# A recurrent step of seven Strassen products: one x block per pair of steps, and h handed on by quadrants

## The chip, the cores and the metric

One core of a Trainium2 chip runs the whole program in one launch. The metric is the device time of one execution in microseconds; the kernel before was measured three times. Engines: TensorE (PE, with its weight loads PEld) does matmuls into PSUM; VectorE (DVE), ScalarE (ACT) and GpSimd (POOL) do the rest; SyncE (SP) only issues DMAs here. Each engine takes its instructions in order.

## What is computed

Two layers, each with its residual. For 64 sequences, 256 steps and width 1024:

```
xW = x @ Wx + b                        # (64, 256, 1024)
h_t = tanh(h_{t-1} @ Wh + xW[:, t])    # h_{-1} = cond, 256 steps one after another
x = x + h
gate = sigmoid(silu(cond @ W1.T + b1) @ W2.T + b2)
x = x + (x + IHaar(gate * Haar(x)))    # the transform over the steps, and its inverse
```

The gate is one row per sequence, the same for all steps, so the transform is undone by its inverse and the second layer comes to x * (2 + gate). The kernel computes `(x + h) * factor` with `factor` = 2 + gate, step by step. All is float32.

## The kernel before

**Layouts.** There are 64 sequences in two groups of 32. A step's h is held "naturally" as 128 partitions x 512 (partition: a quarter q of the width and a sequence within its group; columns: group and 256 of the width), and transposed, `hT`, as the stationary operand of matmuls. A quadrant is 128 columns (E) of these 512: index 0 to 3 for the blocks a11, a12, a21, a22 of a 2 x 2 split of h. An x tile holds a pair of steps (S = 2) and all 64 sequences, transposed.

**h @ Wh** is one level of Strassen-Winograd: seven products of quadrants by blocks of Wh that are prepared once (`StrassenWeight`). `strassen_sides` makes the four sums s0 to s3 of quadrants of `hT` on VectorE (L223 to L226). `strassen_product(out, a, i)` (L182 to L201) issues product i: 4 k by 4 column tiles, 16 float32 matmuls that the profile shows as 32 records, on line 193. `h_product` issues them in the order 1, 2, 5, 6, 7, 4, 3. Products 2, 4, 3 accumulate on a PSUM bank `acc` that ScalarE has filled with the step's xW (`put`, L235); the sums `y` and `u` of the others come off the banks `m16` and `m57` by ScalarE (L246, L251) and VectorE (L257, L260). Then, for the whole 512 columns at once, VectorE adds `h = acc + y` (L265), ScalarE takes tanh (L499), VectorE transposes (L500) and makes the sides of the next step.

**x @ Wx** (`XWork`) is done for a pair of steps at a time, each float32 operand split into three parts of fewer bits, with 48 matmuls of 512 columns (line 278): 16 into the banks `mixed0`, `mixed1` (x2 by wx2), 32 into `main0`, `main1` (x1 by wx1, x0 by wx0). Of these, 24 stand behind the products of an odd step (`first`: 16 mixed and 8 main) and 24 behind those of the even step after it (`second`). The split is VectorE's (L119 high bits, L298 x1, L300 x2) and ScalarE's (L306, x0). `take_mixed` brings `mixed` to SBUF by ScalarE (L314) and adds the bias by GpSimd (L315); `finish` adds `main` by VectorE (L352), writes the sum to DRAM (`sum_d`, L356) and reads it back in the layout of h with eight DMAs (`xw`, L362), all issued by SP.

**The rest of a step.** GpSimd adds hT to the x tile (L562) and multiplies by `factor` (L462); after the odd step SP stores the tile (L586) and loads a later x (L115). The first five pairs come before `factor` is known: they are parked in DRAM (`kept`), and brought back, multiplied and stored later, one half tile in eight steps (`again`).

**The last steps.** The pair 127 gets its xW by plain float32 products in the layout of h, in four pieces beside steps 251 to 254 (`tail_step`, from the weights that `raw_again` puts together again on VectorE), and the last two steps are handled in halves (`pieces`) and added to x and multiplied by VectorE in the transposed layout.

**What sets the order.** TensorE's instructions are issued in the order of the program all through (`manual_schedule`); those of VectorE and ScalarE up to step 1, after which a planner orders them, GpSimd and SP by its own costs. DMAs issued by SP wait for their data in SP's queue, so a waiting one holds those behind it.

Of the kernel before, what the change touches and what calls it, by code (L numbers as in the profile page):

```python
# [52 lines left out]
F32 = mybir.dt.float32  # L53
# [7 lines left out]
P = 128  # L61
R = 32
# [10 lines left out]
HIGH = -(1 << 12)  # L73
UP = float(1 << 12)
DOWN = 1.0 / UP
WARM = 9
LATE = 3
AHEAD = 2
RINGS = 1024


@with_exitstack
def tile_cond_resid(
    ctx: ExitStack,
    tc: tile.TileContext,
    xT: bass.AP,
    condT: bass.AP,
    wx: bass.AP,
    wh: bass.AP,
# [130 lines left out]
    def strassen_sides(hT, t: int):  # L220
        a11, a12, a21, a22 = (hT[:, i * E : (i + 1) * E] for i in range(4))
        s = sums.tile([P, 4, E], F32, tag="s", name=f"s{t}")
        nc.vector.tensor_sub(s[:, 2], a11, a21)  # L223
        nc.vector.tensor_add(s[:, 0], a21, a22)  # L224
        nc.vector.tensor_sub(s[:, 1], s[:, 0], a11)  # L225
        nc.vector.tensor_sub(s[:, 3], a12, s[:, 1])  # L226
        return {1: a11, 2: a12, 3: s[:, 3], 4: a22, 5: s[:, 0], 6: s[:, 1], 7: s[:, 2]}
# [10 lines left out]
    def h_product(acc, a: dict, t: int):  # L238

        m16, m57 = (bank(f"m{i}", f"m{i}_{t}") for i in (16, 57))  # L240
        m16, m5, m7 = m16[:, :E], m57[:, :E], m57[:, E : 2 * E]
        part = [acc[:, i * E : (i + 1) * E] for i in range(3)]
        y = sums.tile([P, 4, E], F32, tag="y", name=f"y{t}")
        u = sums.tile([P, E], F32, tag="u", name=f"u{t}")
        strassen_product(m16, a[1], 1, True)
        nc.scalar.copy(y[:, 0], m16)  # L246

        strassen_product(part[0], a[2], 2) if t != S else None
        strassen_product(m5, a[5], 5, True)
        strassen_product(m16, a[6], 6)  # L250
        nc.scalar.copy(u, m16)  # L251
        strassen_product(m7, a[7], 7)
        strassen_product(part[0], a[2], 2) if t == S else None
        if t == 1:
            for k in range(B - 2, B):
                gate_block(k)
        nc.vector.tensor_add(  # L257
            y[:, 1:3], m57[:, : 2 * E].rearrange("p (i e) -> p i e", i=2), u[:].unsqueeze(1).broadcast_to((P, 2, E))
        )
        nc.vector.tensor_add(y[:, 3], m7, y[:, 1])  # L260
        strassen_product(part[2], a[4], 4)
        strassen_product(part[1], a[3], 3)
        h = work.tile([P, W], F32, tag="h", bufs=1, name=f"h{t}")
        for v in pieces(t):
            nc.vector.tensor_add(h[:, v], acc[:, v], flat(y)[:, v])  # L265
        return h

    def pieces(t: int) -> list:


        return [slice(F, W), slice(0, F)] if t + S >= T else [slice(0, W)]

    def bank(tag: str, name: str):
        return one_pool.tile([P, HALF], F32, tag=tag, name=name)
# [11 lines left out]
    class XWork:  # L286
# [14 lines left out]
                out=self.x2, in0=self.x1[:].bitcast(F32), scalar=-UP, in1=self.high, op0=ALU.mult, op1=ALU.add  # L301
            )

        def begin(self) -> None:
            self.x0 = split.tile([P, D], F32R, tag="x0", name=f"x0_{self.i}")
            nc.scalar.copy(self.x0, self.high)  # L306
            self.mixed = [bank(f"mixed{h}", f"mixed{h}_{self.i}") for h in range(2)]
            self.main = [bank(f"main{h}", f"main{h}_{self.i}") for h in range(2)]

# [7 lines left out]
        def block(self, k: int) -> None:  # L317
# [5 lines left out]
            for h in range(2):  # L323
                x_matmul(self.main, self.x1, 1, h, k, stop=True)

        def first(self) -> None:
            self.begin()

            def low() -> None:
                for k in range(B):  # L330
                    x_matmul(self.main, self.x1, 1, 0, k, start=True)


            low() if self.i == 2 else None
            for h in range(2):
                for k in range(B):
                    x_matmul(self.mixed, self.x2, 2, h, k, True, True)
            self.take_mixed()
            low() if self.i > 2 else None
# [79 lines left out]
    for k in range(B):  # L419
        x_block(k)  # L420
        split_block(k)
        if k == 0:
            now = XWork(1)
            now.split()
            now.begin()
        if k in (3, 5):
            now.block(k // 4)
# [13 lines left out]
        return g1T  # L441

    def gate_factor(z):
        nc.vector.tensor_add(z, gate_ps, z)
        nc.scalar.activation(z, z, AF.Sigmoid)
        factor = const.tile([P, W], F32, tag="factor", name="factor")
        nc.vector.transpose(factor, z)
        nc.vector.tensor_scalar_add(factor, factor, 2.0)  # L448
        return factor
# [15 lines left out]
    nc.vector.tensor_add(h, acc, b_n)  # L465

    tail = {T - 5: [range(3)] * 2, T - 4: [range(3, 5)] * 2, T - 3: [range(5, B), []], T - 2: [[], range(5, B)]}  # L470
    wx_again, ends = [], []

    def raw_again(k: int) -> None:
        wx_again.append(wpool.tile([P, D], F32, tag="wx2", name=f"wx_again{k}"))
        w0, w1 = (wx_s[k][j][:].bitcast(F32) for j in range(2))
        tc.keep_in_program_order(
            nc.vector.scalar_tensor_tensor(out=wx_again[k], in0=w1, scalar=DOWN, in1=w0, op0=ALU.mult, op1=ALU.add)
        )

    def tail_step(t: int) -> None:  # L480
        if not ends:
            for r in range(S):
                ends.append(bank(f"mixed{r}", f"acc{T - S + r}"))
                nc.scalar.copy(ends[r], b_end)
        for r, ks in enumerate(tail[t]):
            for k in ks:
                plain_product(ends[r], pairs[NP - 1], wx_again[k], k, lambda g: (k * S + r) * N + g * R, False, False)


    kept, again, factor = [], [], None  # L490
    for t in range(T):
        i, s = divmod(t, S)
        if s == 0 and t:
            xw = xw_next
        if t:
            h = h_product(acc, sides, t)
        hT = work.tile([P, W], F32, tag="hT", name=f"hT{t}")
        for v in pieces(t):
            nc.scalar.activation(h[:, v], h[:, v], AF.Tanh)  # L499
            nc.vector.transpose(hT[:, v], h[:, v])  # L500
        if t + 1 < T:
            sides = strassen_sides(hT, t)
        if t == 0:
            acc = bank("acc", "acc1")
            nc.vector.tensor_add(acc, acc1, b_n)
# [15 lines left out]
            later.split()  # L521

        elif s == 0:
            if i + 1 < NP:
                acc = put(xw[1], t + 1)
            if i + 2 < NP:
                now.second()
                if i + 3 < NP:
                    later = XWork(i + 2)
                    later.split()  # L530
                xw_next = now.finish()
        if s == 1 and i + 3 < NP:
            now = later
            now.first()
        if s == 1 and i + 2 < NP:
            acc = put(xw_next[0], t + 1)
        if t in tail:
            tail_step(t)

        if T - 7 <= t < T - 3:  # L540
            for k in ((0, 1, 2), (3, 4), (5, 6), (7,))[t - T + 7]:
                raw_again(k)
        if t == T - 16:
            b_end = load_bias(b.rearrange("o (q f) -> (o q) f", q=Q), const, "spare", "b_end")
        if t >= T - 3 and t < T - 1:
            acc = ends[t - T + 3]
        if t == 1:
            in_order.close()
        if t == 2:
# [5 lines left out]
        if t == 0:  # L555
            hT0 = hT
        elif t == 1:

            for r, v in enumerate((hT0, hT)):
                tc.keep_in_program_order(nc.gpsimd.tensor_add(of_step(x, r), of_step(x, r), blocks(v)))  # L560
        elif t + S < T:
            nc.gpsimd.tensor_add(of_step(x, s), of_step(x, s), blocks(hT))  # L562
        if LATE <= t < LATE + B:
            k = t - LATE
# [3 lines left out]
            nc.sync.dma_start(out=w2, in_=w2T[k])  # L568
            plain_product(gate_ps, g1T, w2, k)
            if k == B - 1:  # L570
                factor = gate_factor(b2_n)
        if t + S >= T:

            if s == 0:
                last = slab("last")
            for g, queue in zip((1, 0), (nc.scalar, nc.sync)):
                v = of_step(x, s)[:, g]
                nc.vector.tensor_add(v, v, blocks(hT)[:, g])
                part = slice(s * W + g * F, s * W + (g + 1) * F)
                out = last[:, part].rearrange("p (b m) -> p b m", b=B)  # L580
                nc.vector.tensor_mul(out, v, blocks(factor)[:, g])
                queue.dma_start(out=yT[i][:, part], in_=last[:, part])
        elif factor is not None:
            scale(x, s)
            if s == S - 1:
                nc.sync.dma_start(out=yT[i], in_=x)  # L586
        elif s == S - 1:
            kept.append(dram.tile([P, D], F32, tag="kept", bufs=(LATE + B) // S, name=f"kept{i}"))
            nc.sync.dma_start(out=kept[i], in_=x)
        if s == S - 1:  # L590
            del pairs[i]
            if i + 3 < NP:
                load_x(i + 3)


        if t >= 2 * B and t % 4 == 3 and kept:
# [8 lines left out]
                tc.keep_in_program_order(nc.sync.dma_start(out=by_block, in_=at(kept[j])))  # L605
            else:
                v = again[:].rearrange("p (b g m) -> p g b m", b=B, g=G)
                tc.keep_in_program_order(nc.gpsimd.tensor_mul(v, v, blocks(factor)))
                nc.sync.dma_start(out=at(yT[j]), in_=by_block)
                if (j + 1, r + 1) == (len(kept), S):  # L610
                    kept = []
# [31 lines left out]
```

## Time and profile before

| | us |
|---|---|
| median of three runs | 3089.21 (3089.11 to 3089.31) |
| the profiled execution, device time | 3086.83 |
| its span, first to last instruction | 3085.0 |
| TensorE busy | 3077.1 |
| VectorE busy | 1763.5 |
| GpSimd busy | 1113.6 |
| ScalarE busy | 714.2 |
| half a pair (one step and 24 x matmuls), median of 228 | 11.913 |

A timeline row is: start in us from the span's start, length in us, engine, line, operation, output tile <- input tiles, shapes, count; in brackets the idle time of the engine before it and what ended it. Consecutive instructions of one kind are merged into one row. A matmul's end is modelled, so rows of matmuls overlap; their starts tell the pace. A group row (by line) gives busy time and mean length in ns, then the idle time in front and its releaser.

### The profile page before, as it was taken

How to read it: one execution, taken by the hardware profiler on the slowest of the kernel's cores; microseconds unless marked ns; L12 is line 12 of the kernel's file. 1: busy time of each engine (PE TensorE's matmuls, PEld its weight loads, DVE VectorE, ACT ScalarE, POOL GpSimd, SP SyncE). 2: the span in 40 equal slices, each digit the busy share in tenths (PEclk: the TensorE clock that was granted, in tenths of full speed). 3: DMA queues.
4: the chain of work that ended last, by engine and by line, in shares of the span. 5: the costliest groups of instructions: out<-in, count | busy, mean ns of one | idle time of the engine just before them, and what ended most of it. 6: DMA issues, size and time to landing. Idle time of an engine off the chain costs nothing.

```text
span 3085.0 us, 138204 instructions
## 1 busy us (share of the span) xinstructions
PE 3077.1 (100%) x64073; PEld 2691.3 (87%) x64073; DVE 1763.5 (57%) x2740; ACT 714.2 (23%) x1420; POOL 1113.6 (36%) x764
## 2 busy tenths in 40 slices
PE   9999999999999999999999999999999999999999
PEld 6888888888888888888888888888888888888888
DVE  7555555555555555555555555555555555555556
ACT  3222222222222222222222222222222222222221
POOL 2233343334333333333333334333333333333332
PEclk9999999999999999999999999999999999999999
DMA  7332333232332232222223222222222222222221
GB/s 260 125 101 92 100 96 99 91 103 92 98 98 93 96 97 96 94 91 84 96 86 98 84 92 91 91 91 92 91 92 90 91 91 91 91 87 92 94 78 58
DMA packets 164034, 299.13 MB, mean 97 GB/s; under 512 B 44160, under 2 KB 110336, under 8 KB 163456
## 3 DMA queue, kind: packets, MB, share of 16 engines
q1 hardware_dynamic: 163024, 289.50, 27.7%
q8 instruction: 501, 8.21, 1.1%
q10 hardware_dynamic: 432, 0.79, 0.1%
q14 instruction: 77, 0.63, 0.1%
HBM read 154.40 MB, written 135.79 MB: 94 GB/s over the span
## 4 chain that ended last, share of the span: by engine, by line
PE 98%; DMA 1%; DVE 0%; POOL 0%; SPq 0%; ACT 0%; issue 0%; DVEq 0%; ACTq 0%
PE main L278 30%; PE m L193 30%; PE acc L193 22%; PE mixed L278 16%; PE acc L210 0%; DMA h0T<-condT 0%; DMA wh<-wh 0%; DMA w<-w1T 0%; PE gate_ps L210 0%; POOL sum L315 0%; DMA x<-xT 0%; DMA b_row<-b 0%; DVE hT L500 0%; DVE s L225 0%; DVE s L224 0%; DVE x L298 0%
## 5 line engine op out<-in xcount | busy, mean ns | idle before, releaser
L562 POOL TENSOR_TENSOR x<-x,hT 128x512 f32<-128x512 f32 x252 | 448.0, 1778 | 1696.7 <-DVE hT L500 1676.0
L278 PE MATMUL main<-wx,x 128*128 128x512 f32 x4032 | 973.4, 393 | 0.2 <-DVE x L298 0.2
L278 PEld LDWEIGHTS main<-wx,x 128*128 128x128 f32 x4032 | 746.7, 188 | 177.4 <-issue 26.4
L257 DVE TENSOR_TENSOR y<-m,u 128x256 f32<-128x256 f32 x255 | 108.1, 424 | 847.0 <-PE m L193 847.0
L278 PE MATMUL mixed<-wx,x 128*128 128x512 f32 x2016 | 495.0, 397 | 0.0
L193 PE MATMUL m<-t,s 128*32 128x128 f32 x16320 | 492.6, 273 | 0.2 <-DVE s L225 0.2
L278 PEld LDWEIGHTS mixed<-wx,x 128*128 128x128 f32 x2016 | 368.8, 188 | 96.9 <-issue 24.6
L193 PEld LDWEIGHTS m<-t,s 128*32 128x32 f32 x16320 | 450.8, 110 | 0.5 <-issue 0.4
L315 POOL TENSOR_TENSOR sum<-sum,b_row 128x512 f32<-128x512 f32 x252 | 329.9, 1310 | 240.5 <-ACT sum L314 189.4
L499 ACT ACTIVATE h<-h 128x512 f32<-128x512 f32 (+1 forms) x258 | 162.5, 631 | 790.8 <-DVE h L265 790.8
L462 POOL TENSOR_TENSOR x<-x,factor 128x512 f32<-128x512 f32 x244 | 330.7, 1355 | 15.4 <-DVE factor L448 5.7
L265 DVE TENSOR_TENSOR h<-acc,y 128x512 f32<-128x512 f32 (+1 forms) x257 | 176.5, 687 | 235.1 <-PE acc L193 234.9
L500 DVE STREAM_TRANSPOSE hT<-h 128x512 f32<-128x512 f32 (+1 forms) x258 | 182.4, 707 | 204.0 <-ACT h L499 204.0
L193 PEld LDWEIGHTS m<-wh,hT 128*32 128x32 f32 x8160 | 208.7, 109 | 87.3 <-issue 83.5
L300 DVE SCALAR_TENSOR_TENSOR x<-x,x_high 128x1024 fp32r<-128x1024 f32 x126 | 282.7, 2244 | 0.1
L193 PE MATMUL m<-wh,hT 128*32 128x128 f32 x8160 | 275.5, 275 | 0.0
L193 PE MATMUL acc<-wh,s 128*32 128x128 f32 x8160 | 269.8, 273 | 0.0
L193 PE MATMUL acc<-t,hT 128*32 128x128 f32 x8160 | 269.7, 273 | 0.0
L193 PE MATMUL acc<-wh,hT 128*32 128x128 f32 x8160 | 269.6, 273 | 0.0
L193 PE MATMUL m<-wh,s 128*32 128x128 f32 x8160 | 269.6, 273 | 0.0
L306 ACT CAST x<-x_high 128x1024 fp32r<-128x1024 f32 x126 | 132.1, 1049 | 462.0 <-PE main L278 461.9
L193 PEld LDWEIGHTS acc<-t,hT 128*32 128x32 f32 x8160 | 228.3, 110 | 0.2
(60 smaller groups left out, 2346.2 us busy)
## 6 DMA issues: line engine op xcount, KB each, us to landing
x<-xT SPq DMA_DIRECT2D x127, 512.0 KB, 3.8
sum_d<-sum SPq DMA_DIRECT2D x126, 512.0 KB, 2.9
xw<-sum_d SPq DMA_DIRECT2D x1008, 64.0 KB, 2.0
yT<-x SPq DMA_DIRECT2D x122, 512.0 KB, 3.6
wh<-wh SPq DMA_DIRECT2D x8, 512.0 KB, 11.0
w<-w1T SPq DMA_DIRECT2D x8, 512.0 KB, 8.7
w<-w2T SPq DMA_DIRECT2D x8, 512.0 KB, 4.2
wx<-wx SPq DMA_DIRECT2D x7, 512.0 KB, 8.6
```

The costliest lines, as they stand in the source:

```text
L193: nc.tensor.matmul(out=out[q * R : (q + 1) * R], lhsT=a[:, k * R : (k + 1) * R], rhs=wh_s.sides[i][k][:, q], start=first and k == 0, stop= ...
L257: nc.vector.tensor_add(y[:, 1:3], m57[:, : 2 * E].rearrange("p (i e) -> p i e", i=2), u[:].unsqueeze(1).broadcast_to((P, 2, E)))
L265: nc.vector.tensor_add(h[:, v], acc[:, v], flat(y)[:, v])
L278: nc.tensor.matmul(out=acc[h], lhsT=v[:, k * P : (k + 1) * P], rhs=wx_s[k][which][:, h * HALF : (h + 1) * HALF], start=start and k == 0, s ...
L300: nc.vector.scalar_tensor_tensor(out=self.x2, in0=self.x1[:].bitcast(F32), scalar=-UP, in1=self.high, op0=ALU.mult, op1=ALU.add)
L306: nc.scalar.copy(self.x0, self.high)
L315: nc.gpsimd.tensor_add(s, s, b_row[:, h * HALF : (h + 1) * HALF])
L462: nc.gpsimd.tensor_mul(of_step(x, s), of_step(x, s), blocks(factor))
L499: nc.scalar.activation(h[:, v], h[:, v], AF.Tanh)
L500: nc.vector.transpose(hT[:, v], h[:, v])
L562: nc.gpsimd.tensor_add(of_step(x, s), of_step(x, s), blocks(hT))
```

## The change

- From step 12 (`ALONE` = 3 + 8 + 1) on there is another loop. All 48 x matmuls of a pair (`whole`) stand behind the products of the odd step, in `beside_x`; behind those of the even step the products of the odd step follow at once.
- In that loop the products come in the order 1, 4, 2, 5, 6, 7, 3, with five and seven in the banks `main0` and `main1` (which the x block uses in between) and products 2, 3 and 4 in three banks of their own (`acc`, `m57`, `gate`), each filled by ScalarE with a quadrant of xW (`put_part`) during the step before. Quadrant 3 gets its xW on VectorE.
- h, its tanh and its transpose are taken by quadrants of 128 columns: 0 after product 2, then 3 and 2 after product 7, and 1 after product 3.
- VectorE, ScalarE and GpSimd follow the order of the program there; SP is still ordered by the planner. GpSimd's additions and multiplications of both steps of a pair stand behind the odd step.
- The plain products of the last pair, `raw_again`, `tail_step` and `pieces` go; pair 127 is an x block like the others. The last step stays in natural layout: x of that step is a further input `xN`, multiplied by factor beforehand, so that the end is h * factor + x_n.
- Warm-up matmuls at the start: 6 for 9. `strassen_sides` makes s0 before s2. The cast of x0 is a method of its own (`cast`).

```diff
-WARM = 9
+WARM = 6
+ALONE = LATE + B + 1
@@ strassen_sides
+        nc.vector.tensor_add(s[:, 0], a21, a22)
         nc.vector.tensor_sub(s[:, 2], a11, a21)
-        nc.vector.tensor_add(s[:, 0], a21, a22)
@@ XWork
+        def whole(self) -> None:
+            self.begin()
+            for h in range(2):
+                for k in range(B):
+                    x_matmul(self.mixed, self.x2, 2, h, k, True, True)
+            for h in range(2):
+                for k in range(B):
+                    x_matmul(self.main, self.x1, 1, h, k, start=True)
+            for h in range(2):
+                for k in range(B):
+                    x_matmul(self.main, self.x0, 0, h, k, stop=True)
@@ the loop over steps
-    for t in range(T):
+    for t in range(ALONE):
...
+    def put_part(t: int, j: int):
+        part = bank(("acc", "m57", "gate")[j], f"acc{t}_{j}")[:, :E]
+        nc.scalar.copy(part, xws[t // S][t % S][:, j])
+        return part
+
+    def beside_x(t: int, steps: list) -> None:
+        i = t // S
+        x = pairs[i]
+        if i + 2 < NP:
+            later.whole()
+        for r, v in steps:
+            nc.gpsimd.tensor_add(of_step(x, r), of_step(x, r), blocks(v))
+        if i + 2 < NP:
+            later.take_mixed()
+        for r, _ in reversed(steps):
+            scale(x, r)
+        nc.sync.dma_start(out=yT[i], in_=x)
+        del pairs[i]
+        if i + 4 < NP:
+            load_x(i + 4)
+        nxt = None
+        if i + 3 < NP:
+            nxt = XWork(i + 3)
+            nxt.split()
+        if i + 2 < NP:
+            xws[i + 2] = later.finish()
+        return nxt
...
+    for t in range(ALONE, T):
...
+        m16, m5, m7 = (bank(tag, f"{tag}_h{t}")[:, :E] for tag in ("m16", "main0", "main1"))
...
+        strassen_product(m16, sides[1], 1, True)
+        nc.scalar.copy(y[:, 0], m16)
+        if s == 0 and later is not None:
+            later.cast()
+        strassen_product(accs[2], sides[4], 4)
+        strassen_product(accs[0], sides[2], 2)
+        strassen_product(m5, sides[5], 5, True)
+        nc.vector.tensor_add(quad(h, 0), accs[0], y[:, 0])
+        tanh(0)
+        nc.vector.tensor_add(y[:, 3], m5, xw[:, 3])
+        transpose(0)
+        if final:
+            times_factor(slice(0, E))
+            plus_x(slice(0, E))
+        put_next(0)
+        strassen_product(m16, sides[6], 6)
+        nc.scalar.copy(u, m16)
+        nc.vector.tensor_add(y[:, 3], y[:, 3], u)
+        nc.vector.tensor_add(y[:, 2], accs[2], u)
+        put_next(2)
+        strassen_product(m7, sides[7], 7, True)
+        for o in (3, 2):
+            nc.vector.tensor_add(quad(h, o), m7, y[:, o])
+        tanh(3)
+        tanh(2)
+        nc.vector.tensor_add(y[:, 1], m5, u)
+        transpose(3)
+        strassen_product(accs[1], sides[3], 3)
+        nc.vector.tensor_add(quad(h, 1), accs[1], y[:, 1])
+        tanh(1)
+        if final:
+            times_factor(slice(F, W))
+            times_factor(slice(E, F))
+            plus_x(slice(E, F))
+            plus_x(slice(F, W))
+            break
+        transpose(2)
+        put_next(1)
+        transpose(1)
+        accs = nxt
+        sides = strassen_sides(hT, t)
...
+        if s == 1:
+            later = beside_x(t, [(1, hT), (0, before)])
```

## The prediction

> **What bounds the kernel now.** I read the page's busy times and its chain of waits first, then the timeline of TensorE over two pairs in mid-run, then that of the other engines there, the start and the tail.
>
> ```profile
> PE 3077.1 (100%) x64073; PEld 2691.3 (87%) x64073; DVE 1763.5 (57%) x2740; ACT 714.2 (23%) x1420; POOL 1113.6 (36%) x764
> ...
> PE 98%; DMA 1%; DVE 0%; POOL 0%; SPq 0%; ACT 0%; issue 0%; DVEq 0%; ACTq 0%
> ```
>
> TensorE is the chain; nothing else ends it in mid-run. So the time moves only if TensorE gets through a pair of steps in less time, or starts to wait.
>
> ```profile
> 1509.14 1.08 PE L193 MATMUL m<-wh,hT 128*32 128x128 f32 x32
> 1510.04 1.06 PE L193 MATMUL acc<-wh,hT 128*32 128x128 f32 x32
> 1510.91 1.93 PE L193 MATMUL m<-t,s 128*32 128x128 f32 x64
> 1512.66 1.06 PE L193 MATMUL m<-wh,s 128*32 128x128 f32 x32
> 1513.54 1.06 PE L193 MATMUL acc<-t,hT 128*32 128x128 f32 x32
> 1514.41 1.06 PE L193 MATMUL acc<-wh,s 128*32 128x128 f32 x32
> 1515.39 3.92 PE L278 MATMUL mixed<-wx,x 128*128 128x512 f32 x16
> 1519.15 1.98 PE L278 MATMUL main<-wx,x 128*128 128x512 f32 x8
> 1521.06 1.08 PE L193 MATMUL m<-wh,hT 128*32 128x128 f32 x32
> ```
>
> Read the starts, not the durations. One product of h (32 records) takes 0.873 us start to start (1510.04 to 1514.41 is five), seven take 6.11; but from the first product to the first x matmul it is 6.25. The 24 x matmuls take 5.67 to the next product. Inside a block the records of single matmuls stand 0.2276 us apart, so 24 are 5.46. An excursion from h to x and back thus costs 0.14 + 0.20 us that is no work; from the records exactly: a half pair is 11.913, the work 6.113 + 5.462, the rest 0.338 us. There are two excursions per pair of steps.
>
> ```profile
> 1503.62 0.69 DVE L265 TENSOR_TENSOR h<-acc,y 128x512 f32<-128x512 f32 x1 [0.93 <-PE acc L193]
> 1504.40 0.64 ACT L499 ACTIVATE h<-h 128x512 f32<-128x512 f32 x1 [3.08 <-DVE h L265]
> 1505.14 0.71 DVE L500 STREAM_TRANSPOSE hT<-h 128x512 f32<-128x512 f32 x1 [0.83 <-ACT h L499]
> ...
> 1517.73 0.29 DVE L223 TENSOR_TENSOR s<-hT 128x128 f32<-128x128 f32 x1
> 1517.78 1.40 POOL L562 TENSOR_TENSOR x<-x,hT 128x512 f32<-128x512 f32 x1 [8.16 <-DVE hT L500]
> 1517.94 1.38 DVE L224 TENSOR_TENSOR s<-hT 128x128 f32<-128x128 f32 x1
> ```
>
> This is what the x block covers today: from the last product (its last matmul starts at 1503.28) to a transposed h at 1505.85 nothing of the next step can start, 2.6 us. And an addition of two SBUF tiles on VectorE stands behind a running GpSimd one: 1.38 instead of 0.29 us.
>
> ```profile
> 1512.32 0.32 SPq L356 DMA_DIRECT2D sum_d<-sum  x1
> ...
> 1515.30 3.87 SPq L362 DMA_DIRECT2D xw<-sum_d  x8
> ...
> 1518.74 0.59 ACT L235 COPY acc<-xw 128x512 f32<-128x512 f32 x1 [1.79 <-DMA xw<-sum_d]
> ...
> 1522.48 0.36 SPq L586 DMA_DIRECT2D yT<-x  x1
> ...
> 1526.02 0.35 SPq L115 DMA_DIRECT2D x<-xT  x1
> ```
>
> The way of xW through DRAM takes 6.4 us from the issue of sum_d to the first xw tile in use, and SP's load of x waits 3.2 us for the yT store to land, holding what is queued behind it.
>
> **The change, part by part.**
>
> *One x block per pair.* Excursions per pair go from two to one: 0.338 us for each of XWork 7 to 126, 120 x 0.338 = 40.6 us gained, if TensorE finds its operands at the boundary that loses its x block (even step to odd step). The block itself only doubles: 48 x 0.2276 + 0.338 = 11.26 us.
>
> *That boundary.* Time 0 is the first matmul of product 1 of the even step; new order 1, 4, 2, 5, 6, 7, 3, each 0.873. Latencies from rows: a product's end to ScalarE's copy 0.30 (product 1 gives way to the next at 1510.04, L246 starts at 1510.35; L251 the same), to VectorE 0.25 (L265) to 0.32 (L257); VectorE to ScalarE 0.09; ScalarE to VectorE 0.10; VectorE to the next weight load 0.055 (transpose to product 1 at 3063.6) to 0.12. Sizes: VectorE 128 wide out of PSUM 0.29 (L260), independent ones 0.21 apart (1517.73 to 1517.94); ScalarE copy of 128 0.27 (L251); tanh 0.634 for 512 and 0.409 for 256, so 0.30 for 128; transpose 0.711 and 0.423, so 0.28.
> Product 6 ends 4.37; u copied 4.67-4.94; two additions of u 5.04 and 5.25 to 5.54; put of quadrant 2 on ScalarE until 5.90. Product 7 ends 5.24: h3 at 5.56-5.85, h2 5.77, y1 5.98-6.27. tanh of 3 5.94-6.24, transpose 6.34-6.62. Product 4 of the odd step starts at 6.98 and would load its weights at 6.87; it can from 6.68: 0.2 us spare. Product 3 ends 6.11: h1 behind that transpose at 6.55-6.84, tanh 6.93-7.23, transpose 7.33-7.61, weights from 7.67; product 2 wants them at 7.75: 0.08 spare. s0 is ready at 7.84, product 5 wants it at 8.62; s1, s3 follow with more. So I put this wait at 0. Bounds: the spare is smaller than the error of seven added rows, each within 0.07 (the small semaphore instruction that stands before some of them); from below 0, as products already follow without a gap; from above 0.4 us (49 us in all), if most of the seven are late. I take 0, since the rows' sum fits and the 0.09 and 0.10 already hold such an instruction.
>
> [...] The rows show 0.21 apart at a length of 0.29. [...]
>
> *Work moved beside the x block.* GpSimd's eight operations of a pair (two additions of h 1.4, two of the bias 1.28, two by factor 1.27; 7.9 us, every fourth pair one more of 1.28) start when the odd step's h is transposed, 1.4 us into the block. Alternating with VectorE's sides (4 x 0.29), high bits (0.68), x1 (1.18, after the x1 matmuls at 7.9) and x2 (1.1), GpSimd is done near 10.5, x2 near 11.5, the two sums out of main (0.68 each) near 12.9, that is 1.6 us into the even step; its first addition is due at 2.9, product 5 writes main0 at 2.6. If each alternation is worse, 2.7: still covered. In records where an addition out of PSUM ran beside GpSimd (L257, 10 times) it kept its 0.42, so the sums aren't held.
>
> *SP.* Worst order: yT at 10.5, the x load behind its landing at 14.1, sum_d at 14.5, xw in use at 20.9 into the block. It is first needed by ScalarE's put in the odd step, 11.26 + 6.11 + 3.6 = 21.0. Behind that put stands the copy of u (due 1.1 later), and behind that only the chain of the odd step, covered by the next block. Cost 0.
>
> *Smaller parts.* ScalarE's puts (3 x 0.27 for 0.59) and quarter tanhs raise it to about 3.7 us of 11.7 per step: covered. The cast moves behind y0's copy in the even step (1.05 us, done at 2.5, tanh due at 3.2). VectorE's s0 before s2 changes no sum, its wx_again (8 x 1.2) goes where it wasn't waited for; xN comes, b_end's loads go: one-offs off the chain. *Warm-up 9 to 6*: single records show matmuls of x_block at half pace until 9.37 us, 8.2 us after the first. Three fewer let 1.8 us of cold work start earlier, worth 0.9; but at 54.59 the x block waits for VectorE's x1 (54.54), whose queue mostly doesn't hang on TensorE: I take 0.3 of 0 to 0.9. [...]
>
> *Tail.* The four plain blocks (3040.24-3045.42, 3051.53-3054.99, 3061.10-3063.69, 3070.24-3072.83) are 13.8 us, one more x block is 11.3: -2.5. A stall of 0.44 in step 254 goes. The last product's end to the end of the span is 6.06 now; in natural layout h1, tanh, times factor, plus x, two issues: 2.45, then 2.3 as now from the last issue: 4.75, -1.3. Between steps 253 and 254 no x block is left while GpSimd runs: s2 and s1 each wait 1.1 to 1.3, product 6 stalls: +1.0 (0 to 2).
>
> **Sum**: 40.6 + 0.3 + 2.5 + 0.4 + 1.3 - 1.0 = 44.1. The profiled execution took 3086.83 (span 3085.0); 3042.7 on its terms. The median of the three runs lies 2.4 above it, so 3045. Steps 12 onward hold 122 boundaries of even to odd, which is what a wait there is multiplied by.
>
> **Rivals.**
> *The boundary is exposed.* For it: 0.08 us spare. Against: the sums fit. At 0.1 to 0.3 us per boundary, 3057 to 3082, still faster.
> *The same, past its tipping point.* From 44.1 / 122 = 0.36 us per boundary the gain is gone; at 0.5 it is 3106. For that, quadrant 1 must come at 8.25 instead of 7.67; VectorE's four-piece chain (h3, transpose 3, h1, transpose 1) would have to be 0.15 late in each piece. No row of that length shows it.
> *The loop through SP and DRAM binds.* xw late, ScalarE's put late, the odd step's h late, GpSimd late, yT late, sum_d late again: a ring that fits into 23.49 us with some 1.1 us spare. If GpSimd and VectorE hold one another for 1.5 us longer than now, the ring is 23.9 and the time 3045 + 122 x 0.4 = 3094: slower. It decides from 23.85.
> *The merge saves nothing*: the 0.338 isn't the excursion but returns elsewhere, as a slow first product. 3086. Against: 226 excursions show the same 0.203 and 0.318 at the two ends.
>
> **How the numbers follow.** Likeliest (3041 to 3049): 0.66. Boundary partly exposed: 0.16. Past the tipping point: 0.07. The ring: 0.05. No saving: 0.04. Something at start or hand-over of a few us: 0.02. Within 0.2% (6 us, about what a measurement here can tell) lies the fourth and the rims: 0.03. Faster 0.84, slower 0.13. The range goes from 3040 (no stall at 253, all the warm-up) into the exposed boundary, to 3080.
>
> **What the profile after would show.** Rows of 16 and 32 L278-like matmuls only once per 23.49 us; product 1 of the odd step 0.873 after product 3 of the even; no idle before weight loads there, above all none released by VectorE's transposes; VectorE's addition for quadrant 0 starting 2.9 into the even step. Wrong it goes if weight loads of products 4 or 2 of odd steps show idle time, if ScalarE waits long for xw, or if the odd step's first product comes late.

## The result, and the profile after

| | before | after |
|---|---|---|
| median, us | 3089.26 (3089.11 to 3089.33) | 3302.91 (3296.76 to 3309.60) |
| the profiled execution, and its span | 3086.83, 3085.0 | 3309.6, 3307.5 |
| a pair of steps, first x matmul to first x matmul, median (for before two halves) | 23.83 | 25.47 (90th percentile 28.21) |
| sum_d, from its issue to its landing, median | 2.9 | 5.3 |

The ratio is 1.0692 (95% interval 1.0671 to 1.0714): slower by 214 us, where 44 less were forecast. Busy times and the chain of waits from the page of after:

```profile
PE 3113.0 (94%) x63862; PEld 2710.4 (82%) x63862; DVE 2166.9 (66%) x4683; ACT 839.9 (25%) x2641; POOL 1270.6 (38%) x766
...
q8 instruction: 500, 8.19, 1.1%
...
issue 29%; PE 25%; POOL 15%; DVE 14%; DMA 14%; SPq 2%; ACT 1%; DVEq 0%; ACTq 0%; POOLq 0%
DMA sum_d<-sum 8%; POOL x L476 7%; PE main L274 6%; PE acc L195 6%; PE main_h L195 5%; POOL x L590 4%; PE m_h L195 4%; POOL sum L313 3%; DMA xw<-sum_d 3%; DVE x L294 3%; PE mixed L274 3%; DVE x_high L121 2%; SPq L374 2%; DVE s L227 2%; DVE s L228 2%
```

Before, PE was 98% of the chain. Now it is a quarter, and the rest is shared by GpSimd, VectorE, DMAs (sum_d first) and "issue", time in which an engine waited for nothing that the profile shows. A chain that goes through so many engines suggests a ring, in which each waits for the one before. The timeline of after, TensorE over a pair:

```profile
1506.71 1.06 PE L195 MATMUL acc<-wh,s 128*32 128x128 f32 x32
1507.59 1.06 PE L195 MATMUL m_h<-wh,hT 128*32 128x128 f32 x32
1508.46 1.06 PE L195 MATMUL acc<-t,hT 128*32 128x128 f32 x32
...
1512.83 0.40 PE L195 MATMUL acc<-wh,s 128*32 128x128 f32 x8
...
1514.49 0.86 PE L195 MATMUL acc<-wh,s 128*32 128x128 f32 x24 [1.26 <-issue]
...
1515.28 3.96 PE L274 MATMUL mixed<-wx,x 128*128 128x512 f32 x16
...
1519.91 7.54 PE L274 MATMUL main<-wx,x 128*128 128x512 f32 x32 [0.67 <-DVE y L666]
...
1527.38 1.08 PE L195 MATMUL m_h<-wh,hT 128*32 128x128 f32 x32
...
1530.72 1.08 PE L195 MATMUL main_h<-t,s 128*32 128x128 f32 x32 [0.51 <-DVE sum L364]
```

The boundary that the prediction doubted holds: from product 3 of the even step to product 1 of the odd one it is 0.88 us (1506.71 to 1507.59), no wait. What stands still is elsewhere: inside a product (1.26, "issue"), before the main matmuls of the x block, which write the banks of products 5 and 7 and so wait for the odd step's last use of them, and before product 5 of the next even step, which waits for the sum out of main. The same stretch on the queues, ScalarE, VectorE and GpSimd:

```profile
1499.83 4.50 POOL L476 TENSOR_TENSOR x<-x,factor 128x512 f32<-128x512 f32 x2
...
1504.36 0.36 SPq L595 DMA_DIRECT2D yT<-x  x1
...
1507.40 0.35 SPq L117 DMA_DIRECT2D x<-xT  x1
...
1507.84 0.38 SPq L368 DMA_DIRECT2D sum_d<-sum  x1
...
1513.16 4.70 SPq L374 DMA_DIRECT2D xw<-sum_d  x8
...
1518.18 0.27 ACT L580 COPY acc<-xw 128x128 f32<-128x128 f32 x1 [7.02 <-DMA xw<-sum_d]
1518.38 0.26 ACT L657 COPY u<-m_h 128x128 f32<-128x128 f32 x1
1518.68 0.29 DVE L658 TENSOR_TENSOR y<-y,u 128x128 f32<-128x128 f32 x1 [6.84 <-ACT u L657]
...
1521.00 2.76 POOL L590 TENSOR_TENSOR x<-x,hT 128x512 f32<-128x512 f32 x2 [16.67 <-DVE hT L627]
...
1526.71 4.49 POOL L476 TENSOR_TENSOR x<-x,factor 128x512 f32<-128x512 f32 x2
...
1531.22 0.36 SPq L595 DMA_DIRECT2D yT<-x  x1
```

Read it as a loop. SP's yT waits for GpSimd's multiplication (done 1504.33). The load of x waits for yT to land (1507.40). sum_d stands behind both, lands 5.3 us later, xw follows, and ScalarE's put, which stood idle for 7.02 us with the copy of u behind it, goes at 1518.18. So the odd step's transposed h is there only 5.7 us into its x block of 12.1, GpSimd begins at 1521.00, is done at 1531.20, and SP's next yT goes at 1531.22: 26.86 us after the one before. It is the ring of the third rival, closed. The landing times in the page, SP's issues:

```profile
x<-xT SPq DMA_DIRECT2D x127, 512.0 KB, 4.4
sum_d<-sum SPq DMA_DIRECT2D x127, 512.0 KB, 5.3
xw<-sum_d SPq DMA_DIRECT2D x1016, 64.0 KB, 2.0
yT<-x SPq DMA_DIRECT2D x122, 512.0 KB, 2.8
```

Most of the 2.4 us that sum_d takes longer goes with the 512 KB of x issued 0.44 us ahead of it: with that load moved behind it, it takes 3.4 (below). Last, the waits of after (engine, line, what it waited for, us in total, times, longest):

```profile
ACT acc L580 <- DMA xw<-sum_d: 635.1, 112, 9.7
...
PEld main_h L195 <- DVE sum L364: 79.6, 92, 1.9
PE main L274 <- DVE y L666: 79.4, 72, 2.8
PEld main L274 <- issue: 74.4, 48, 3.1
...
PE main_h L195 <- DVE sum L364: 54.9, 91, 1.7
...
PE acc L195 <- issue: 27.3, 32, 2.2
...
PE main_h L195 <- issue: 20.1, 13, 2.5
```

So in this trace TensorE itself waits more for the ring (79.4 and 54.9) than in "issue" gaps (27.3 and 20.1).

The "issue" gaps have a pattern in the trace's packets. The page lists a queue "q8 instruction": 500 packets, 8.19 MB, so 16 KB each, which is one for some 128 of the 63862 matmul records. That it brings TensorE's instructions is the author's inference from its name and this count. In a stretch of h (0.0273 us per matmul) 128 matmuls take 3.5 us. Such a packet began at 1512.15 and took 0.96; TensorE went on at 1514.49, 1.38 after its end. In before, where every 6.1 us of h is followed by 5.7 us of x (24 matmuls), no such gap is to be seen: 240 half pairs, from first product to first product, lie between 11.913 and 11.980.

A smaller loss stands beside the long gaps. The granted clock of after, 0.995 in the mean, is 1.00 but for nine stretches of 3.41 us in mid-run, in which it is 0.50. Each of the nine lies at a gap of 2.2 to 2.9 us between two matmuls; 13 other gaps of 2.2 us or more in this trace have no such stretch, so the gap alone doesn't tell. The first one in the windows of the trace, and the matmul there:

```profile
311.41:314.82 3.41, 3.23 (x8) 2.58 (x9) 3.21 (x9) 1.66 (x5) 2.09 (x2) 0.50 0.34 77
...
311.59 4.73 PE L274 MATMUL main<-wx,x 128*128 128x512 f32 x13 [2.51 <-DVE y L666]
```

The x matmuls there stand 0.427 us apart instead of 0.2276. Nine such stretches are 31 us at a granted clock of 0.50, by an estimate some 15 us of work lost. Before has none in mid-run.

Two suspects, then: the ring (sum_d behind yT and the load of x), and, as a theory of the author's, instruction fetches held up by data, mostly by the 1.5 MB that SP issues within 3.5 us (yT, x, sum_d). Both hang on the order of SP.

### The profile page after: what moved, and what is told of

Its sections match the earlier page's. It is cut to its first block, busy times and chain, and to the rows that moved or that the text cites. A ratio compares the mean times of both kernels' runs of the same rounds, so it can differ in the third digit from the quotient of the medians.

```text
span 3307.5 us, 141547 instructions
## 1 busy us (share of the span) xinstructions
PE 3113.0 (94%) x63862; PEld 2710.4 (82%) x63862; DVE 2166.9 (66%) x4683; ACT 839.9 (25%) x2641; POOL 1270.6 (38%) x766
## 3 DMA queue, kind: packets, MB, share of 16 engines
q8 instruction: 500, 8.19, 1.1%
## 4 chain that ended last, share of the span: by engine, by line
issue 29%; PE 25%; POOL 15%; DVE 14%; DMA 14%; SPq 2%; ACT 1%; DVEq 0%; ACTq 0%; POOLq 0%
DMA sum_d<-sum 8%; POOL x L476 7%; PE main L274 6%; PE acc L195 6%; PE main_h L195 5%; POOL x L590 4%; PE m_h L195 4%; POOL sum L313 3%; DMA xw<-sum_d 3%; DVE x L294 3%; PE mixed L274 3%; DVE x_high L121 2%; SPq L374 2%; DVE s L227 2%; DVE s L228 2%
## 5 line engine op out<-in xcount | busy, mean ns | idle before, releaser
L274 PE MATMUL main<-wx,x 128*128 128x512 f32 x4064 | 961.1, 393 | 81.6 <-DVE y L666 79.4
L476 POOL TENSOR_TENSOR x<-x,factor 128x512 f32<-128x512 f32 x244 | 531.6, 2198 | 5.8 <-DVE factor L462 5.7
L623 ACT ACTIVATE h<-h 128x128 f32<-128x128 f32 x976 | 275.7, 306 | 530.6 <-DVE h L648 427.0
L580 ACT COPY acc<-xw 128x128 f32<-128x128 f32 x732 | 193.5, 265 | 806.1 <-DMA xw<-sum_d 635.1
L195 PE MATMUL main_h<-t,s 128*32 128x128 f32 x7808 | 266.6, 274 | 60.8 <-DVE sum L364 54.9
L627 DVE STREAM_TRANSPOSE hT<-h 128x128 f32<-128x128 f32 x972 | 296.9, 305 | 39.4 <-ACT h L623 39.4
L195 PEld LDWEIGHTS main_h<-t,s 128*32 128x32 f32 x7808 | 215.0, 110 | 87.5 <-DVE sum L364 79.6
L195 PE MATMUL main_h<-wh,s 128*32 128x128 f32 x7808 | 269.1, 273 | 14.6 <-issue 14.3
L294 DVE TENSOR_TENSOR x<-x,x_high 128x1024 fp32r<-128x1024 f32 x127 | 258.9, 2038 | 24.4 <-PE main L274 13.1
L195 PE MATMUL m_h<-t,s 128*32 128x128 f32 x7808 | 267.0, 273 | 2.7 <-issue 2.6
L195 PE MATMUL m_h<-wh,hT 128*32 128x128 f32 x7808 | 262.8, 274 | 0.4 <-issue 0.3
```

What stands on the lines that cost most here:

```text
L195: nc.tensor.matmul(out=out[q * R : (q + 1) * R], lhsT=a[:, k * R : (k + 1) * R], rhs=wh_s.sides[i][k][:, q], start=first and k == 0, stop= ...
L274: nc.tensor.matmul(out=acc[h], lhsT=v[:, k * P : (k + 1) * P], rhs=wx_s[k][which][:, h * HALF : (h + 1) * HALF], start=start and k == 0, s ...
L294: nc.vector.tensor_sub(self.x1, x, self.high)
L476: nc.gpsimd.tensor_mul(of_step(x, s), of_step(x, s), blocks(factor))
L580: nc.scalar.copy(part, xws[t // S][t % S][:, j])
L623: nc.scalar.activation(quad(h, j), quad(h, j), AF.Tanh)
```

## The experiments

All start from the kernel after. Times of before in the same runs were 3087.97 to 3088.43.

**The ring cut at ScalarE.** In odd steps the three copies of xW into banks stand behind the last tanh, so that a late xw holds nothing but the copies.

```diff
-        put_next(0)
+        put_next(0) if s == 0 else None
...
-        put_next(2)
+        put_next(2) if s == 0 else None
...
         transpose(2)
-        put_next(1)
+        for part_j in (1,) if s == 0 else (2, 0, 1):
+            put_next(part_j)
```

> The changed kernel, but in odd steps ScalarE fills the three banks of the next step after its tanh of quadrant 1 instead of between its other work, so that a late xw holds nothing of the odd step. Ring theory (late xw -> ScalarE's put -> late h of the odd step -> late GpSimd and VectorE -> late sum_d -> late xw): the ring is cut, the odd step's h is done about 1.4 us into the x block, the waits for main and for product 5 of the even step go, 3050 to 3120. Lock theory (VectorE and GpSimd hold one another, and the x split and the sums out of main come late by themselves): the wait of product 5 stays at 0.7 us per pair, 3200 or more. Instruction-fetch theory (two h steps in a row use up instructions faster than they come): no change, 3280 to 3310.

Measured: 3208.96 us (ratio 1.0396, 1.0380 to 1.0411), 94 less than after. The chain is TensorE again (96%, issue 4%), and the waits for L364 and L666 are gone. So the ring was closed and cost some 94 us; but more than half of the loss is left, with TensorE as the chain. Timeline of this kernel, SP and TensorE at the start of an odd step:

```profile
1521.85 0.35 SPq L117 DMA_DIRECT2D x<-xT  x1
...
1522.29 0.38 SPq L368 DMA_DIRECT2D sum_d<-sum  x1
...
1525.42 1.06 PE L195 MATMUL m_h<-wh,hT 128*32 128x128 f32 x32
1526.29 0.62 PE L195 MATMUL acc<-t,hT 128*32 128x128 f32 x16
1529.19 0.91 PE L195 MATMUL acc<-t,hT 128*32 128x128 f32 x16 [2.28 <-issue]
```

The packets of x and sum_d keep the DMA engines 70% to 100% busy from 1523.0 to 1527.0. The next instruction packet begins at 1527.01, right behind them, takes 0.96, and TensorE goes on 1.2 later: 2.28 us lost. With the ring cut, such gaps are what TensorE loses: 125 over 0.25 us, 145 us in all, where the trace of after has 69 with 71 us beside the ring's waits. Ten stretches at a granted clock of 0.50 are left too.

**SP's order: sum_d and xw first.** sum_d, the eight xw, yT, the load of x. The load, no longer issued by the planner as early as a tile is free, takes a tile that has been free for long, and so waits for no landing.

```diff
-        nc.sync.dma_start(out=yT[i], in_=x)
-        del pairs[i]
-        if i + 4 < NP:
-            load_x(i + 4)
...
             xws[i + 2] = later.finish()
+        tc.keep_in_program_order(nc.sync.dma_start(out=yT[i], in_=x))
+        del pairs[i]
+        if i + 4 < NP:
+            pairs[i + 4] = slab(f"x{i + 4}")
+            tc.keep_in_program_order(nc.sync.dma_start(out=pairs[i + 4], in_=xT[i + 4]))
```

> The changed kernel, but SP issues sum_d and the eight xw loads ahead of the yT store and the x load of the pair, so that sum_d waits for no landing and no x load runs beside it. Ring theory: sum_d lands in about 2.9 us instead of 5.3 and is issued up to 3.4 us sooner, the ring fits into a pair again, 3050 to 3120. Lock theory: sum_d is still late by VectorE, 3200 or more. Instruction-fetch theory: the stalls inside products stay unless they come from the x load's burst; 3230 to 3300.

Measured: 3060.06 us (ratio 0.9907, 0.9892 to 0.9922): 243 less than after and faster than before, by the order of 11 DMAs and the tile that the load takes. The median pair is 23.47. sum_d lands in 3.2. The rest above 23.47, summed over 120 pairs, is 20 us, against 268 in after. It is the order that before already has in the rows that the prediction shows (sum_d 1512.32, xw 1515.30, yT 1522.48, x 1526.02).

**Both.** The two edits together.

> Both edits. Ring theory: no better than the better one of the two by more than 20 us, 3045 to 3110. Lock theory: 3200. Instruction-fetch theory: what is left above 3045 are stalls that the profile puts down to no releaser, in the second half of the even step and in the odd one.

Measured: 3064.37 us (0.9922, 0.9906 to 0.9939). With the order mended, cutting the ring gains nothing (the time is 4 us longer than with the order alone): it doesn't bind any more.

**What in the order did it?** One run has the order of after (yT, x, sum_d, xw) without the wait for a landing, one moves the load of x alone to the end (yT, sum_d, xw, x).

```diff
-        nc.sync.dma_start(out=yT[i], in_=x)
+        tc.keep_in_program_order(nc.sync.dma_start(out=yT[i], in_=x))
         del pairs[i]
         if i + 4 < NP:
-            load_x(i + 4)
+            pairs[i + 4] = slab(f"x{i + 4}")
+            tc.keep_in_program_order(nc.sync.dma_start(out=pairs[i + 4], in_=xT[i + 4]))
```

> The changed kernel with its SP order kept (yT store, x load, sum_d, xw), but the x load goes into an older buffer, so that it waits for no landing: store, load and sum_d are issued back to back. If the landing wait in SP's queue is what makes sum_d late, 3050 to 3110. If it is the burst (the load's 512 KB ahead of sum_d on the same DMA engines, which also holds back instruction fetches), sum_d still takes 5 us to land and stalls without a releaser stay: 3130 to 3230.

Measured: 3194.09 us (1.0343, 1.0328 to 1.0359), 109 less than after. The ring is open here (PE is 97% of the chain) and yet sum_d still takes 5.1 us to land and the median pair is 24.56, with "issue" gaps. The wait for the landing is not the greater part.

```diff
-        nc.sync.dma_start(out=yT[i], in_=x)
+        tc.keep_in_program_order(nc.sync.dma_start(out=yT[i], in_=x))
         del pairs[i]
-        if i + 4 < NP:
-            load_x(i + 4)
...
             xws[i + 2] = later.finish()
+        if i + 4 < NP:
+            pairs[i + 4] = slab(f"x{i + 4}")
+            tc.keep_in_program_order(nc.sync.dma_start(out=pairs[i + 4], in_=xT[i + 4]))
```

> The changed kernel, but the x load alone goes behind the xw loads; the yT store stays ahead of sum_d. Both accounts of the x load (its wait, its bytes) say that sum_d lands in about 3 us and the time is near that of the second experiment, 3050 to 3080. If the store is as harmful as the load, 3130 or more.

Measured: 3078.65 us (0.9968, 0.9957 to 0.9980), 224 less than after; sum_d lands in 3.4. So the place of one DMA per pair, the load of x between yT and sum_d, made 224 of the 243 us. The page's rows of sum_d in the three orders (yT, x, sum_d without the wait; yT, sum_d, x; sum_d first):

```profile
sum_d<-sum SPq DMA_DIRECT2D x127, 512.0 KB, 5.1
```

```profile
sum_d<-sum SPq DMA_DIRECT2D x127, 512.0 KB, 3.4
```

```profile
sum_d<-sum SPq DMA_DIRECT2D x127, 512.0 KB, 3.2
```

**yT and the load of x out of the steps of h.** ScalarE issues them in the x block (yT of the pair before), SP only sum_d and xw.

```diff
...
+            if parked:
+                j, done = parked.pop()
+                nc.scalar.dma_start(out=yT[j], in_=done)
+            if i + 4 < NP:
+                pairs[i + 4] = slab(f"x{i + 4}")
+                nc.scalar.dma_start(out=pairs[i + 4], in_=xT[i + 4])
             later.take_mixed()
...
-        nc.sync.dma_start(out=yT[i], in_=x)
-        del pairs[i]
-        if i + 4 < NP:
-            load_x(i + 4)
+        parked.append((i, pairs.pop(i)))
...
```

> The changed kernel, but store (of the pair before) and x load are issued by ScalarE right behind its work for the odd step's h, so that they run under the x block, where the DMA queues stand idle and TensorE needs few instructions; SP has only sum_d and xw. If the 0.16 us per pair that the second experiment loses against 23.47 us are instruction fetches behind data, they go: 3038 to 3052. If they come from the eight xw loads, no better than 3060. A late ScalarE (0.7 us of issuing) costs nothing in the x block.

Measured: 3066.84 us (0.9928, 0.9912 to 0.9945): no gain on 3060. Gaps of 0.2 to 1.0 us stay, nearly all in odd steps, from their first products on. What remains to move data there is sum_d and xw.

**No sum_d and no xw.** On the run of 3060.

```diff
+            if self.i > ALONE // S + 1:
+                return xws[ALONE // S + 1]
             d = dram.tile([P, D], F32, tag="sum_d", name=f"sum_d{self.i}")
```

> The order sum_d, xw, yT, x load (3060.1) once more, but from XWork 8 on the sums are not written to DRAM nor read back: the steps take their xW from the tiles of pair 7, so the recurrence is fed with the wrong xW and y is not the reference's. Everything else is as it was: the same matmuls, the sums out of main, yT and the load of x. Of the 2 MB that a pair moves, sum_d and xw are half. Theory A: the 15 us that are left above 3045 are instruction fetches of TensorE that queue behind the packets of sum_d and xw. Then the median period stays 23.47, its upper half falls to it, and the time is 3043 to 3050. Theory B: they are the fetches' own length where two steps of h follow each other (16 KB per 3.5 us), whatever else is moved. Then 3056 to 3062.

Measured: 3123.74 us (1.0114, 1.0098 to 1.0131). Half of the traffic is gone and the kernel is 64 us slower, outside both ranges: both theories fall. Timeline of this kernel:

```profile
1182.81 0.35 SPq L603 DMA_DIRECT2D yT<-x  x1
1183.26 0.37 SPq L607 DMA_DIRECT2D x<-xT  x1
...
1186.98 1.05 PE L195 MATMUL m_h<-t,s 128*32 128x128 f32 x30
...
1188.94 0.30 PE L195 MATMUL m_h<-t,s 128*32 128x128 f32 x1 [0.91 <-issue]
```

yT and x, 1 MB without a hole, now begin with the even step: with nothing of sum_d and xw before them on SP they come 11 us earlier within the pair than in the run of 3060. An instruction packet that began at 1186.06, amid them, took 1.54 us (0.96 in the cases above), and TensorE went on 1.34 behind it. In the run of 3060 xw had pushed that megabyte to the end of the odd step and into the x block, where a matmul takes 0.2276 us instead of 0.027: by an estimate from these two, 128 matmuls, a packet's share, last over eight times as long there.

**The odd step's xw last.** On the run of 3060: sum_d, four xw, yT, x, four xw.

```diff
-            for s in range(S):
-                t = xwpool.tile([P, 4, E], F32, tag="xw", name=f"xw{self.i * S + s}")
...
+            for s in range(S if self.i <= ALONE // S else 1):
+                self.load_xw(s)
...
             tc.keep_in_program_order(nc.sync.dma_start(out=pairs[i + 4], in_=xT[i + 4]))
+        if i + 2 < NP:
+            with tc.manual_schedule(engines={mybir.EngineType.SP}):
+                later.load_xw(1)
```

> The same order, but the four xw loads of the odd step, which is due a step and an x block later, go behind yT and the load of x: sum_d, xw of the even step, yT, x load, xw of the odd step. Theory A (fetches queue behind data packets): what counts is how long a burst is without a hole; four of the eight xw loads of the first burst go to the end of the second: 3052 to 3062, with the stalls moved later in the pair. Theory B (the fetches' own length): 3058 to 3062 and the stalls where they were. A time over 3065 would say that the loads of the odd step now come late.

Measured: 3126.42 us (1.0125, 1.0099 to 1.0151). A miss of both theories for the same reason: yT and x, with four xw fewer in front, come 2.8 us earlier, into the odd step. The profiled execution has some loss by late xw too (ScalarE waits 54.8 us for it, 26.8 in the run of 3060), but most of TensorE's loss is in gaps behind instruction packets: 83 over 0.25 us within the steps of h, 63 us in all, against 32 with 14 us in the run of 3060.

The place within the pair goes with the time in most of these runs, though not in all: yT and the load of x by ScalarE stand later than in the run of 3060 and are not faster, and in the first row the ring is closed. SP's or ScalarE's issue, median over the pairs of the trace, in us from the even step's first product (0 to 6.1 the even step, to 12.2 the odd one, then the x block):

| order | sum_d | yT | load of x | time |
|---|---|---|---|---|
| after: yT, x, sum_d, xw | 7.01 | 3.84 | 6.57 | 3302.91 |
| the same without the wait for the landing | 1.62 | -0.68 | -0.28 | 3194.09 |
| sum_d, xw, yT, x, xw | 1.62 | 7.64 | 8.07 | 3126.42 |
| yT, x; no sum_d, no xw | | -0.68 | -0.23 | 3123.74 |
| yT, sum_d, xw, x | 1.62 | -0.66 | 10.30 | 3078.65 |
| yT, x by ScalarE | 1.62 | 12.95 | 13.34 | 3066.84 |
| sum_d, xw, yT, x | 1.62 | 10.35 | 10.97 | 3060.06 |

With yT and x 2.8 us later (7.64 to 10.35) 66 us are gained, and with the load of x alone at 10.30 instead of -0.28, 115.

**Nothing but instructions in the steps of h.** The third theory (what counts is whether a dense stretch of data lies in the steps of h) calls for both edits at once: no sum_d and no xw, and yT and x in the x block by ScalarE.

> Both things at once: nothing through DRAM from XWork 8 on (the steps take the xW of pair 7, so y is not the reference's), and ScalarE issues the yT of the pair before and the load of x in the x block. So no data moves while the products of h run, only instructions. Theory C, formed after the last two runs: TensorE's instruction fetches are held up by whatever dense burst (512 KB or more without a hole) falls into the steps of h; without sum_d and xw the yT and the load of x came some 5 us earlier, out of the last product and the x block into the even step, and so those two runs were slower. Then this one has no stalls left: 3040 to 3050, median period 23.47 and its 90th percentile under 23.6. Theory B, the fetches' own length: 3055 to 3066, with stalls of 0.2 to 0.9 us as in the run with ScalarE's queue (3066.8). Theory A (amount of sum_d and xw) has fallen by the run of 3124.

Measured: 3041.77 us (0.9849, 0.9834 to 0.9864). Windows of the two runs without sum_d and xw (even step, odd step, x block; busy time and records of each engine, clock, share of the DMA engines, GB/s). First yT and x from SP, 3123.74:

```profile
1183.47:1189.60 6.13, 5.22 (x183) 4.95 (x186) 2.39 (x6) 1.90 (x5) 0.00 (x0) 1.00 0.54 174
1189.60:1196.00 6.40, 6.09 (x223) 5.83 (x219) 3.97 (x16) 1.98 (x9) 0.00 (x0) 1.00 0.03 6
1196.00:1207.00 11.00, 11.00 (x100) 9.15 (x93) 8.52 (x16) 2.72 (x8) 8.18 (x6) 1.00 0.01 1
```

Then from ScalarE in the x block, 3041.77:

```profile
1507.43:1513.57 6.14, 6.14 (x225) 6.14 (x228) 3.51 (x11) 2.52 (x8) 0.00 (x0) 1.00 0.01 3
1513.57:1519.80 6.23, 6.23 (x233) 6.03 (x225) 3.97 (x18) 2.38 (x11) 0.00 (x0) 1.00 0.02 5
1519.80:1530.90 11.10, 11.10 (x52) 8.93 (x49) 9.08 (x11) 1.77 (x5) 9.22 (x6) 1.00 0.29 96
```

The work and the bytes are the same; the DMA share of 0.54 in the even step goes to 0.29 in the x block, and TensorE has no gap left. 82 us lie between the two. All pairs but 6 of 120 are under 23.6.

The gaps of all runs have an end in common. In the ten traces after the first, 700 gaps of more than 0.25 us stand between two matmuls of the steps of h, beyond their pace of 0.027; 695 of them end 1.15 to 1.65 us after the end of an instruction packet, whether the gap is short or 3 us long; in the first, that of after, all 69 that no semaphore ended do. Of all matmuls in these steps 9% start that long after one. In these records, then, a gap ends at a steady distance behind a packet, and the run of 3041.77, in which no data moves there, has two such gaps.

**The same with the whole computation, as far as it goes.** sum_d and the even step's xw can't leave the steps of h, since the next odd step copies them; the odd step's xw can: ScalarE issues its four loads in the next x block, ahead of yT and x, and `finish` loads the even step's alone.

```diff
+        while half_read:
+            half_read.pop().load_xw(1, nc.scalar)
         if i + 2 < NP:
             if parked:
                 j, done = parked.pop()
...
             xws[i + 2] = later.finish()
+            half_read.append(later)
```

> The whole computation. ScalarE issues in the x block: the four xw loads of the odd step (of the pair whose sums were written a pair before), the yT of the pair before and the load of x. SP issues sum_d and the four xw loads of the even step alone, behind the products of h. By theory C half of the remaining traffic of xw leaves the steps of h: the stalls at the first products of the odd step get shorter, 3048 to 3062. By theory B it is as before this move, 3062 to 3068. Six issues ahead of ScalarE's copies out of mixed could make those late, and GpSimd's bias, x2 and sum_d after them: then sum_d is issued over 0.5 us later than in the run of 3066.8 and some of the gain goes.

Measured: 3051.84 us (0.9877, 0.9860 to 0.9893), the fastest whole kernel here: 37 less than before and 251 less than after. sum_d is issued 0.15 us later than in the run of 3066.84, so the six issues on ScalarE hold little up. The rest above 23.47 falls to 13 us in 120 pairs (31 in the run of 3066.84).

## Why the prediction was wrong

The predicted 3045 came out as 3302.91, on the other side of before. Step by step:

- **The excursion, 0.338 us for each of 120.** Right in mechanism and size. Where nothing disturbs, a pair takes 23.47 (forecast 23.49), and the run with quiet steps of h reaches 3041.77. The forecast sum of 44.1 measures 46.7 there (3088.43 - 3041.77), with sum_d and xw left out.
- **The boundary, 0.** Right, with spares of 0.08 and 0.2 that were smaller than the error claimed for them: product 1 of the odd step 0.88 behind product 3, product 4 0.87 behind that (1507.59 to 1508.46), product 2 0.87 more. Two sides of the odd step that don't hang on each other (L226, L227) start at 1508.91 and 1509.11, 0.20 apart at a length of 0.28, and no weight load waits there: the 0.21 of the row of before was the right price.
- **GpSimd beside the x block, done near 10.5.** In after it begins late and each multiplication takes 2.2 us instead of 1.27 (two in 4.50). In the quiet run the six operations of a pair (the prediction says eight, but lists and sums six) take 9.3 us, not 7.9: 2.75 for the additions, 3.04 for the bias, 3.51 for the multiplications. It begins 1.2 us into the block and is done at 10.4, and VectorE's sums out of main at 12.7 (forecast 10.5 and 12.9): covered there.
- **SP, "Cost 0": here it failed.** The step put xw in use at 20.9 and its need at 21.0, in what it called the worst order, and wrote 0 for a spare of 0.1. That sum had sum_d land as before, 6.4 us from issue to use. But in the order that it had itself written down the 512 KB of x go right ahead of sum_d, and sum_d lands in 5.3 us instead of 2.9. So the term was 2.4 us late on a spare of 0.1 (1.1 until the copy of u is held), and that closes the ring: a pair takes 25.47 where the rival decides from 23.85. The ring was there as a rival with a chance of 0.05 and a price of 3094 (for 1.5 us); its start was looked for in GpSimd and VectorE, not in the queue. Cutting it at ScalarE gave 94 us back.
- **What no step had: instruction packets move on the DMA engines beside the data** (500 of 16 KB in after, 1.1% of the 16 engines). What is left with the ring opened and TensorE as the chain (3194 and 3209 against 3060) is mostly in gaps of up to 2.9 us behind instruction packets of 16 KB: 127 and 145 us of them in these two traces. The change laid two steps of h end to end, 12.2 us in which 128 matmuls, a packet's share, take 3.5 us, and SP's order put 1.5 MB into just that stretch. The prediction's list of transfers asked when each lands, never what else moves at that time. How the 243 us divide between ring and packets is not exact, since each shifts the other: 94 to 109 went with the ring opened, 134 to 149 are left after it; but in the trace of after itself, gaps counted from matmul to matmul, the ring's two waits take some 160 us, the gaps behind packets 71 and the stretches at a clock of 0.50 some 15, the estimate above. No run has the closed ring without these bursts.
- **Warm-up, 0.3 of 0 to 0.9.** Too small: the x block that began at 54.59 begins at 53.6, 1.0 earlier. The row (half pace until 8.2 us after the first matmul) priced three fewer at 0.9, close to it. Full clock was granted 8.1 us after the first matmul in before and 6.4 in after. In after, gaps before step 12 take it back (the block of step 11 starts at 180.97 in both), in the quiet run it stays (179.89).
- **Tail.** The stall of 1.0 at step 253 doesn't appear in the quiet run: four steps in 24.4 us. The end after the last product is 5.4 there (4.75 forecast, 6.1 before).

Of the ways that the text named for going wrong, "if ScalarE waits long for xw" is what came: 635.1 us.

## What to carry to other kernels

When a change takes breaks out of the bound engine's stream, list the DMAs of each queue in the order in which they will be issued, with bytes, and reprice each landing by what goes right ahead of it; a spare of 0.1 us at the end of a chain of transfers is a risk, not a zero. Put the transfers on which the next step waits first (243 us here). Stores and prefetches belong in the stretch where the bound engine runs few long instructions: 82 us with nothing else moving, though no gain over the mended order with sum_d and all of xw still in the steps of h. An "issue" gap inside a block of equal matmuls asks for a look at the instruction packets: the same matmuls took 3302.91 and 3051.84 us, by where and from which queue 11 DMAs of a pair are issued.

## What the runs showed of the hardware

- An instruction packet of 16 KB took 0.88 to 1.47 us, median 1.00, for 348 of the quiet run that no data overlaps. With the ring cut, two packets' starts lie 8.4 us apart (1518.57 and 1527.01), the second right behind the packets of x and sum_d; 128 matmuls of h, a packet's share, take 3.5. Of 700 gaps in the steps of h 695 end 1.15 to 1.65 us after a packet's end.
- At each of the 25 stretches of 3.41 us at a granted clock of 0.50 (9 in after, 10 with the ring cut at ScalarE, 4 without the wait for the landing, 2 with the odd step's xw last) stands a gap of 2.2 to 3.1 us in TensorE's stream. In after, x matmuls stood 0.427 us apart in one instead of 0.2276, and 13 other gaps of 2.2 us or more have no such stretch.
- Less traffic can be slower: without sum_d and xw 3123.74, with them 3060.06; without them yT and x were issued 11 us earlier within the pair (-0.68 against 10.35).
- The sparse rows of xw (some 65 KB per 0.5 us, 45% of the DMA engines) hurt little: with sum_d and xw alone in the steps of h 31 us in 120 pairs are left above 23.47, and 13 when half of xw leaves them. Packets of x, yT and sum_d fill the engines, some 190 KB per 0.5 us; sum_d alone does so for some 1.5 us.
- What lies in the 1.15 to 1.65 us between a packet's end and TensorE's next matmul, and what sets the granted clock, no run here settles.
